# Two groups instead of three in layer 1, and a denser schedule of gathers and last layernorms

## The chip, the cores and the metric

One core of a Trainium2 chip runs the whole program. Its engines have queues of their own and run beside each other: TensorE (PE; its weight loads are PEld), VectorE (DVE), ScalarE (ACT), GpSimd (POOL) and SyncE (SP), which only starts transfers. Plain DMAs are started from SP and ACT, indirect ones (scatter and gather of rows by an index tensor) from POOL. Each engine takes its instructions in the program's order and waits at the head of its queue. The metric is the device time of one execution in microseconds (us).

## What is computed

Two transformer layers over 16 batches of 512 tokens with 128 channels, all in float32. Each layer is a retention attention and a mixture of eight experts, two of them for every token; after each half a layernorm of the sum with its input:

```python
x = _layernorm(x + _L0_attn_ref(x, ...))
x = _layernorm(x + _L0_ffn_ref(x, ...))   # 8 experts, inner width 256, top 2 per token
x = _layernorm(x + _L1_attn_ref(x, ...))
x = _layernorm(x + _L1_ffn_ref(x, ...))   # 8 experts, inner width 512, top 2 per token
```

The expert half of layer 1, the one that the change touches most, computes for every token only its two experts in the kernel:

```python
top_v, top_i = jax.lax.top_k(xf @ Wg, 2)
top_w = softmax(top_v)
y = einsum('enf,efd->end', silu(xf @ W1) * (xf @ W3), W2)
out = sum(take_along_axis(y, top_i) * top_w)
```

## The kernel before

**Groups, parts, blocks.** The batches of a layer are cut into groups (`PARTS`, line 29: layer 0 has two groups of 8, layer 1 three groups of 6, 8 and 2 batches), and a group into parts of 2 or 3 batches. When the attention of a batch is done, its tokens are routed: eight indirect DMAs (`put` in `route`, line 465) scatter its rows into the group's `rows` in DRAM, where every expert has a region of its own. When a part's batches have been routed, `sort` makes a table of blocks of 128 rows on VectorE, each of one expert, and `experts` runs over them. `_blocks` says how many: a part may leave rows of an expert that do not fill a block to the next part; the last part of a group takes all that are left, and so each group has E - 1 = 7 blocks more than its rows would fill. In layer 1 the groups have 9 + 16 + 30, 17 + 24 + 30 and 23 blocks.

**A block** in `experts` takes three loads on SP's queue (the rows `xb` 64 KB, and in layer 1 the weights `w` 512 KB and `wd` 256 KB), a transpose on TensorE (`turn`, line 1007) with its copy on ScalarE (line 1009), in layer 1 eight matmuls up (line 1024), a silu on ScalarE (1032), a product on VectorE (1033), four matmuls down (1043), a copy on ScalarE (1047) and a store into `results` from ScalarE's queue. Blocks go in pairs, with loads two pairs ahead. In float32 each of the matmuls up and down is two records in the profile.

**Gather and layernorm.** A group's results can be used only when its last part is done: then the places of its rows are known (`places`, VectorE work that is spread over the steps of the last part) and the group is `ready`. For a batch, `gather` asks for eight indirect DMAs into a buffer `yg` (three buffers, `YG`) and loads the kept input `xk` on SP's queue (four buffers). `combined` multiplies by the weights on VectorE (line 1101), adds (1106, 1107) and runs the `layernorm`: statistics, `inv_std` and `nb` on VectorE, four activations on ScalarE (line 340). In layer 0 the result is the input of layer 1's attention; in layer 1 `final` stores it to the output from ScalarE's queue.

**The order of work** is made by the loop at the end of `two_layers`. Three slots hold attentions of batches as generators; `order` fixes which comes next. A round goes once over the slots; for each it takes one step of the attention, one indirect DMA off the queue `moves` (`move`, which makes the DMA wait for the last marked instruction, a copy or silu of ScalarE or a product of VectorE, so that it is paced by these), and steps of `queue[0]`, the experts, as `pace` says. After the slots, `fetch` asks for the next batch's gathers if its group is ready and fewer than 2 (layer 0) or, without attention, 3 (layer 1) batches are held, and one step of the first of `finals` is taken. Where no attention is left (`moved` is false), a round is two steps of the experts, each followed by two indirect DMAs:

```python
        if not moved:
            for _ in range(2):
                step()
                move(now=True)
                move(now=True)
        fetch()
        if finals and next(finals[0], finals) is finals:
            finals.pop(0)
```

A scheduler in the framework then places the instructions on each engine's queue, so that the order on an engine isn't exactly that of the calls.

**`r`** (lines 812 and 947) is the sum that goes into the layernorm behind the attention, with eight columns for the router: `[P, C, DE]`, in the pool `ap` with two buffers. It is written from PSUM (by ScalarE in layer 0, line 819, by VectorE in layer 1, lines 953 and 954) and read until the four activations of line 340.

Of the kernel before, what the change touches and what calls it, by code (L numbers as in the profile page):

```python
# [10 lines left out]
F32 = mybir.dt.float32  # L11
# [7 lines left out]
P = 128  # L19
# [6 lines left out]
OVER = 20  # L26


PARTS = ((2, 2, 2, 2), (2, 2, 2, 2)), ((2, 2, 2), (3, 3, 2), (2,))
WAITS = "for indirect DMAs"  # L30
BK = 128
H0, DK0, DV0 = 4, 32, 64
# [6 lines left out]
def _region(B, T):  # L39

    return BK + max(sum(parts) for layer in PARTS for parts in layer) * T

# [91 lines left out]
def two_layers(  # L134
# [22 lines left out]
    C = T // P  # L157
# [3 lines left out]
    RS = _region(B, T)  # L161
    assert all(sum(sum(parts) for parts in layer) == B for layer in PARTS)

# [3 lines left out]
    ap = ctx.enter_context(tc.tile_pool(name="ap", bufs=2))  # L167
# [29 lines left out]
    DE = D + E  # L197
# [34 lines left out]
    def depends(later, earlier, reason):  # L232
        tc.add_manual_dep(
            later.ins,
            earlier.ins.name,
            mybir.DependencyInfo(mybir.DependencyClass.Sync, mybir.DependencyReason.DATA),
            reason=reason,
        )
# [4 lines left out]
    def move(now=False):  # L243

        some = moves[0] or moves[1]
        if not some or not (marks or now):
            return
        begun = some.popleft()()
        if marks:
            last[:] = marks[-1:]  # L250
            marks.clear()
        if last:
            depends(begun, last[0], "paced by the other engines")
# [39 lines left out]
    def two_banks(name):  # L293

        banks = [psum_a(f"{name}_{k}")[:, : 2 * DE].rearrange("p (c d) -> p c d", d=DE) for k in range(2)]
        return banks, [banks[c // 2][:, c % 2] for c in range(C)]
# [48 lines left out]
    class Group:  # L345


        def __init__(self, l, g, begin):
            self.layer, self.name = l, f"{l}_{g}"
            self.parts = PARTS[l][g]  # L350
            self.begin = begin
# [341 lines left out]
    def attention0(b, xT, group):  # L693
        n = f"a0_{b}"
# [114 lines left out]
        if not sums_of:  # L809
            prepare(0)  # L810
        banks, py = two_banks(f"py_{n}")
        r = ap.tile([P, C, DE], F32, tag="r", name=f"r_{n}")
        for c in range(C):
            at = bass.ts(c, P)
            nc.tensor.matmul(py[c], xT[:, at], same0, start=True, stop=False)
# [13 lines left out]
    def attention1(b, xt, group):  # L829


        n = f"a1_{b}"
# [111 lines left out]
        give("v")  # L944
        yield
        banks, py = two_banks(f"py_{n}")
        r = ap.tile([P, C, DE], F32, tag="r", name=f"r_{n}")
        for c in range(C):
            nc.tensor.matmul(py[c], oT[:, bass.ts(c, P)], w2_sb, start=True, stop=True)
            if c % 2:  # L950
# [117 lines left out]
    def gather(l, b):  # L1068

        group = groups[l, b]  # L1070
        k = b - group.begin
        place = group.place[:, k].rearrange("p k c -> p (k c)")
        y = ap.tile([P, 2, C, D], F32, bufs=YG, tag="yg", name=f"yg_{l}_{b}")
        rows = y.rearrange("p k c d -> p (k c) d")
        here = [0]

        def get(n):
            here[0] += 1
            return nc.gpsimd.indirect_dma_start(  # L1079
                out=rows[:, n],  # L1080
                out_offset=None,
                in_=group.results,
                in_offset=bass.IndirectOffsetOnAxis(ap=place[:, n : n + 1], axis=0),
            )

        moves[1].extend(partial(get, n) for n in range(2 * C))
        xt = xp.tile([P, C, D], F32, bufs=YG + 1, tag="xk", name=f"xk_{l}_{b}")
        nc.sync.dma_start(out=xt.rearrange("p c d -> p (c d)"), in_=kept[l, b])
        return y, xt, here
# [24 lines left out]
    for l in range(2):  # L1114
        b = 0
        for g, parts in enumerate(PARTS[l]):
            begin = b
# [7 lines left out]
    def fetch():  # L1125

        for l, most in ((0, 2), (1, 1 if jobs else YG)):
            b = fetched[l]
            held = sum(1 for k, _ in gathered if k == l)
            if b < B and groups.get((l, b)) in ready and held < most:  # L1130
                gathered[l, b] = gather(l, b)
                fetched[l] += 1

    def attention(l, b):
        group = groups[l, b]
        if l == 0:
            yield from attention0(b, xTs.pop(b), group)
        else:
            while (0, b) not in gathered:
                yield WAITS  # L1140
            x2 = yield from combined(0, b, "x2")
            yield
            yield from attention1(b, x2, group)
# [10 lines left out]

    order = [(0, b) for b in range(sum(PARTS[0][0]) + W)]
    later = [(0, b) for b in range(len(order), B)], [(1, b) for b in range(B)]
# [8 lines left out]
    queue, finals = [], []  # L1165
# [3 lines left out]
    def work(group, part, table, blocks, need):  # L1169
        while len(group.puts) < need:  # L1170
            yield WAITS
        last = part == len(group.parts) - 1
        others = places(group) if last else iter(())
        for _ in experts(group, part, table, blocks, group.puts[:need]):
            next(others, None)
            yield
        for _ in others:
            pass
        if last:
            ready.add(group)  # L1180
            if group.layer == 1:
                finals.append(final(group))
# [8 lines left out]
    def pace():  # L1191


        most, so_far = 0.0, 0
        for l, _, some, group in queue:
            so_far += some
            if l == 0 and len(group.runs) == len(group.parts):
                before = until((1, group.begin), 0) - (W * 2 - 1) * STEPS[0] // 2 - OVER // 2
                most = max(most, so_far / max(before, 1))
        ends = {part_of[n][0]: n for n in order}  # L1200
        coming = [until(n, STEPS[0]) for part, n in ends.items() if left[part]]
        if coming:
            most = max(most, so_far / (min(coming) + OVER))
        return most

    def step():

        if queue:
            got = next(queue[0][1], queue)
            if got is queue:  # L1210
                queue.pop(0)
            elif got is not WAITS:
                queue[0][2] -= 1
# [4 lines left out]
    while jobs or any(slots) or queue or finals:  # L1218
        moved = held = False
        for k in range(W):  # L1220
            if slots[k] is None and jobs and steps >= k * STEPS[0] / W:
                l, b = jobs[0]
                if l == 0 or groups[0, b] in ready:
                    jobs.pop(0)
                    if (l, b) not in groups:
                        (_, g, _), begin = part_of[l, b]
                        group = Group(l, g, begin)
                        for i in range(begin, begin + group.size):
                            groups[l, i] = group
                    slots[k] = ((l, b), attention(l, b))  # L1230
                else:
                    held = True
            if slots[k] is None:
                continue
            moved = True
            steps += 1
            move()
            (l, b), gen = slots[k]
            got = next(gen, slots)
            todo[l, b] = max(todo[l, b] - 1, 1)  # L1240
            if got is WAITS or len(moves[0]) + len(moves[1]) > 2 * C:
                move(now=True)
            if got is slots:
                slots[k] = None
                todo[l, b] = 0
                part, _ = part_of[l, b]
                left[part] -= 1
                if not left[part]:
                    group = groups[l, b]
                    i, table, blocks, need = sort(group)  # L1250
                    at = 1
                    while at < len(queue) and queue[at][0] <= l:
                        at += 1
                    some = (blocks + 1) // 2 + (blocks if l else (blocks + 1) // 2)
                    queue.insert(at, [l, work(group, i, table, blocks, need), some, group])
            owed += pace()
            while queue and owed >= 1.0:
                owed -= 1.0
                step()
            if not queue:  # L1260
                owed = 0.0
        if held:
            step()
        if not moved:
            for _ in range(2):
                step()
                move(now=True)
                move(now=True)
        fetch()
        if finals and next(finals[0], finals) is finals:  # L1270
            finals.pop(0)


_OUT = "out_dram"
# [69 lines left out]
```

## Time and profile before

| what | value |
|---|---|
| median of 13 executions | 1500.35 us (1492.54 to 1514.79) |
| the profiled execution | 1502.49 us |
| its span in the profile | 1500.4 us, 34347 instructions |
| TensorE busy | 1286.5 us (86%) |
| weight loads busy | 1120.0 us (75%) |
| VectorE busy | 966.5 us (64%) |
| ScalarE busy | 546.6 us (36%) |
| GpSimd busy | 507.0 us (34%) |
| DMA | 277.36 MB, mean 185 GB/s |
| indirect scatters (line 465) | 256, 999 ns each |
| indirect gathers (line 1079) | 256, 977 ns each |

The profile is one execution. Its busy times are means over stages that differ, so it is read by stages: the part with 40 slices shows which engine is busy when, the stretches in microseconds show it finer, the timeline of one engine gives each instruction with the idle time before it and what ended this, and the groups by line give the mean time of an instruction. A wait for several things is put down to the one that came last. Names in the views have their numbers left out, so `yg` stands for the buffers of all batches; `rout` is `results`, `rin` is `rows`.

### The profile page before, as it was taken

Reading aid. Unit: us, or ns where it says so; the run is one execution under the profiler, and the core shown is the slowest. Engines: PE = TensorE matmul, PEld = TensorE weight load, DVE = VectorE, ACT = ScalarE, POOL = GpSimd, SP = SyncE. Lnnn points to the kernel's source line nnn. Section 1 sums busy time; section 2 is a strip of 40 time slices with the busy share of each in tenths; the row PEclk is TensorE's granted clock in tenths of the full one; section 3 lists DMA queues with packets and bytes.
Section 4 is the critical chain, followed back from the end, with each engine's and each line's share of the span. In section 5 each row is a group of like instructions: output and inputs, shape, how many; then the busy total and the mean of one; then the engine's idle time right before and its main releaser. Section 6 shows DMA issues by size and latency. Waiting matters only on the chain.

```text
span 1500.4 us, 34347 instructions
## 1 busy us (share of the span) xinstructions
PE 1286.5 (86%) x11230; PEld 1120.0 (75%) x11230; DVE 966.5 (64%) x4134; ACT 546.6 (36%) x1344; POOL 507.0 (34%) x519
## 2 busy tenths in 40 slices
PE   6878799999879989879999889999999988887850
PEld 4757678788756868767788779888888987776740
DVE  4685778846665868786658755675877881112465
ACT  3333344434333434514434342452444332222231
POOL 0041320420264341632434523352565340005564
PEclk9889899999989999989999999999999999998985
DMA  5024255566553443627676765775787797788862
GB/s 167 8 85 125 72 159 158 167 194 192 168 164 104 130 123 113 197 69 209 190 254 215 229 206 182 245 238 176 237 266 231 246 304 263 258 254 265 261 200 70
DMA packets 208914, 277.36 MB, mean 185 GB/s; under 512 B 26976, under 2 KB 133728, under 8 KB 208608
## 3 DMA queue, kind: packets, MB, share of 16 engines
q1 hardware_dynamic: 134336, 205.59, 43.9%
q10 hardware_dynamic: 58016, 36.00, 7.7%
q0 software_dynamic: 16384, 33.59, 6.9%
q8 instruction: 89, 1.46, 0.4%
q14 instruction: 89, 0.73, 0.2%
HBM read 224.02 MB, written 51.05 MB: 183 GB/s over the span
## 4 chain that ended last, share of the span: by engine, by line
PE 59%; DVE 15%; DMA 10%; issue 6%; POOL 4%; ACT 3%; SPq 2%; ACTq 0%; POOLq 0%; DVEq 0%
PE pgu L1024 19%; PE py L1043 10%; DMA xb<-rin 5%; POOL yg L1079 4%; PE po_a L778 4%; PE pb_a L707 3%; PE psc_a L656 3%; PE po_a L911 2%; PE pt L1007 2%; DMA yg<-rout,place 2%; PE pa_a L705 2%; DVE sc_a L660 2%; PE py_a L817 2%; PE po_a L770 2%; PE pa_a L847 1%
## 5 line engine op out<-in xcount | busy, mean ns | idle before, releaser
L1024 PE MATMUL pgu<-xbT,w 128*128 128x128 f32 x3520 | 465.2, 285 | 33.4 <-ACT xbT L1009 31.7
L1024 PEld LDWEIGHTS pgu<-xbT,w 128*128 128x128 f32 x3520 | 439.3, 200 | 49.9 <-ACT xbT L1009 39.3
L465 POOL DMA_INDIRECT rin<-x,at_f x256 | 255.8, 999 | 590.1 <-ACT yb L1047 98.5
L1079 POOL DMA_INDIRECT yg<-rout,place x256 | 250.2, 977 | 389.5 <-DMA xb<-rin 136.9
L1033 DVE TENSOR_TENSOR h<-sg,pgu 128x512 f32<-128x512 f32 (+1 forms) x221 | 150.8, 682 | 279.6 <-PE pgu L1024 265.9
L1043 PE MATMUL py<-wd,h 128*128 128x128 f32 x1760 | 242.9, 284 | 18.0 <-ACT xbT L1009 8.0
L1043 PEld LDWEIGHTS py<-wd,h 128*128 128x128 f32 x1760 | 217.1, 194 | 40.2 <-ACT xbT L1009 13.6
L1032 ACT ACTIVATE sg<-pgu 128x512 f32<-128x512 f32 (+1 forms) x221 | 131.3, 594 | 200.9 <-PE pgu L1024 191.4
L660 DVE TENSOR_TENSOR sc_a<-psc_a,cs 128x512 f32<-128x512 f32 x192 | 119.6, 682 | 29.1 <-PE psc_a L656 28.8
L1047 ACT COPY yb<-py 128x256 f32<-128x256 f32 (+1 forms) x148 | 54.4, 368 | 210.7 <-PE py L1043 206.4
L1007 PE MATMUL pt<-cs,xb 128*128 128x128 f32 x291 | 82.3, 297 | 39.2 <-DMA xb<-rin 34.8
L1009 ACT COPY xbT<-pt 128x256 f32<-128x256 f32 (+1 forms) x148 | 54.5, 368 | 124.4 <-PE pt L1007 112.3
L1007 PEld LDWEIGHTS pt<-cs,xb 128*128 128x128 f32 x291 | 41.4, 147 | 59.3 <-DMA xb<-rin 42.3
L778 PEld LDWEIGHTS po_a<-v_a,sc_a 128*128 128x128 f32 x512 | 71.8, 203 | 10.8 <-DVE sc_a L660 5.9
L340 ACT ACTIVATE y_c<-yg,nb_y_c,rs_y_c 128x128 f32<-128x128 f32 x128 | 54.3, 484 | 58.1 <-DVE nb_y_c L334 57.9
L778 PE MATMUL po_a<-v_a,sc_a 128*128 128x64 f32 x512 | 70.8, 279 | 4.4 <-DVE sc_a L660 4.4
L707 PE MATMUL pb_a<-w_in_sb,xT 128*128 128x512 f32 x128 | 70.5, 634 | 0.0
L340 ACT ACTIVATE x<-r_a,nb_x,rs_x 128x128 f32<-128x128 f32 x128 | 54.0, 485 | 20.4 <-DVE nb_x L334 10.3
L786 DVE TENSOR_TENSOR og_a<-po_a,sg_a 128x256 f32<-128x256 f32 x64 | 27.0, 422 | 47.8 <-ACT sq_a L785 47.2
L1101 DVE TENSOR_TENSOR yg<-yg,gw 128x1024 f32<-128x1024 f32 x32 | 39.2, 1226 | 26.2 <-DMA yg<-rout,place 24.8
L656 PE MATMUL psc_a<-qkT_a,kk_a 32*128 32x128 f32 x1024 | 52.9, 290 | 3.0 <-DVE sc_a L660 1.2
L705 PE MATMUL pa_a<-w_in_sb,xT 128*128 128x256 f32 x128 | 42.7, 417 | 13.2 <-DMA w_in_sb<-in_w_in_dram 10.8
(198 smaller groups left out, 1942.6 us busy)
## 6 DMA issues: line engine op xcount, KB each, us to landing
w<-in_ex_dram SPq DMA_DIRECT2D x149, 512.0 KB
wd<-in_ex_dram SPq DMA_DIRECT2D x149, 256.0 KB
w<-in_ex_dram SPq DMA_DIRECT2D x142, 256.0 KB
xb<-rin SPq DMA_DIRECT2D x291, 64.0 KB
rout<-yb ACTq DMA_DIRECT2D x143, 128.0 KB
wd<-in_ex_dram SPq DMA_DIRECT2D x142, 128.0 KB
kept<-x ACTq DMA_DIRECT2D x32, 256.0 KB
xk<-kept SPq DMA_DIRECT2D x32, 256.0 KB
```

Of the source, the lines that this page charges most:

```text
L340: nc.scalar.activation(y[:, c, :], r[:, c, :D], AF.Identity, bias=nb[:, c : c + 1], scale=rs[:, c : c + 1])
L465: moved = nc.gpsimd.indirect_dma_start(out=group.rows, out_offset=bass.IndirectOffsetOnAxis(ap=at[:, n : n + 1], axis=0), in_=xt[:, n % C, :],
L656: nc.tensor.matmul(banks[r][i], kT(r, i), qT(r, i), start=True, stop=True)
L660: return nc.vector.tensor_tensor(sc[:, r], bank.rearrange("p (c t) -> p c t", t=P), causal[:, None, :].to_broadcast([P, C, P]), ALU.mult,)
L707: nc.tensor.matmul(pb, lhsT, w_in0_sb[:, 2 * P :], start=True, stop=True)
L778: nc.tensor.matmul(po[:, h * DV0 : (h + 1) * DV0], sc[:, h, c], v[:, c, h * DV0 : (h + 1) * DV0], start=c == 0, stop=c == 0 or h == H0 - 1,)
L1007: nc.tensor.transpose(pt[:, k], loaded_[i][0], ident)
L1024: nc.tensor.matmul(bank[:, m * nf + f], loaded_[i][1][:, k * F + f * P : k * F + (f + 1) * P], turned[i], start=True, stop=True,)
L1032: mark(nc.scalar.activation(sg, banks[0], AF.Silu))
L1033: nc.vector.tensor_tensor(h, sg, banks[1], ALU.mult)
L1043: nc.tensor.matmul(py[:, m], h[:, f], wd[:, f * P : (f + 1) * P], start=f == 0, stop=f == nf - 1)
L1079: return nc.gpsimd.indirect_dma_start(out=rows[:, n], out_offset=None, in_=group.results, in_offset=bass.IndirectOffsetOnAxis(ap=place[:, ...
```

## The change

Layer 1 has one group of 14 batches, with the parts 2, 2, 2, 3, 3, 2, and one of 2 batches. Its blocks are 9 + 16 + 16 + 24 + 24 + 30 and 23. The region of an expert in `rows` grows with the largest group (`_region`), for both layers. `r` has one buffer. Where no attention is left, each of a round's two expert steps is followed by three indirect DMAs and a `fetch`, and a round takes three steps of the last layernorms instead of one.

```diff
-PARTS = ((2, 2, 2, 2), (2, 2, 2, 2)), ((2, 2, 2), (3, 3, 2), (2,))
+PARTS = ((2, 2, 2, 2), (2, 2, 2, 2)), ((2, 2, 2, 3, 3, 2), (2,))
...
-        r = ap.tile([P, C, DE], F32, tag="r", name=f"r_{n}")
+        r = ap.tile([P, C, DE], F32, bufs=1, tag="r", name=f"r_{n}")
...
-        r = ap.tile([P, C, DE], F32, tag="r", name=f"r_{n}")
+        r = ap.tile([P, C, DE], F32, bufs=1, tag="r", name=f"r_{n}")
...
         if not moved:
             for _ in range(2):
                 step()
-                move(now=True)
-                move(now=True)
+                for _ in range(3):
+                    move(now=True)
+                fetch()
         fetch()
-        if finals and next(finals[0], finals) is finals:
-            finals.pop(0)
+        for _ in range(1 if moved else 3):
+            if finals and next(finals[0], finals) is finals:
+                finals.pop(0)
```

## The prediction

> **What bounds the kernel now.** First the page's second part, the span in 40 slices, to see where the engines change places:
>
> ```profile
> PE   6878799999879989879999889999999988887850
> ...
> POOL 0041320420264341632434523352565340005564
> ```
>
> TensorE is at 90% or more through most of the span. GpSimd is at a third, has nothing at all in slices 34 to 36, and works on at the end, where TensorE has run dry. So the last stages were cut out with the busy times by stretch (columns: stretch, its length, then PE, PEld, DVE, ACT, POOL busy with counts, TensorE's clock, DMA share, GB/s):
>
> ```profile
> 1075.00:1125.00 50.00, 46.24 (x455) 41.08 (x455) 40.24 (x155) 19.62 (x46) 31.74 (x33) 1.00 0.77 251
> 1125.00:1175.00 50.00, 49.64 (x563) 43.31 (x562) 39.16 (x149) 20.23 (x52) 26.66 (x28) 1.00 0.72 230
> 1175.00:1235.00 60.00, 54.12 (x464) 51.95 (x463) 51.10 (x258) 24.01 (x56) 25.20 (x26) 1.00 0.90 288
> 1235.00:1355.00 120.00, 101.05 (x838) 94.80 (x837) 22.70 (x33) 32.71 (x68) 0.00 (x0) 1.00 0.80 258
> 1355.00:1449.00 94.00, 72.11 (x545) 66.74 (x542) 38.66 (x116) 26.80 (x61) 51.77 (x52) 0.93 0.80 260
> 1449.00:1500.40 51.40, 0.00 (x0) 0.00 (x0) 32.93 (x137) 9.97 (x25) 28.92 (x29) 0.51 0.26 79
> ```
>
> Three stages: until 1235 attention, experts and the final layernorms of group 1_0's six batches lie together, TensorE 150.0 of 160 us busy. From 1235 to 1355 the last 30 blocks of group 1_1 run alone. From 1355 the gathers of 1_1 and 1_2 run, at first beside the 23 blocks of 1_2, from 1449 with TensorE idle. GpSimd's timeline of that end (start, duration, what, idle before and its releaser):
>
> ```profile
> 1355.41 0.97 POOL L1079 DMA_INDIRECT yg<-rout,place  x1 [122.62 <-DMA xb<-rin]
> 1356.69 0.96 POOL L1079 DMA_INDIRECT yg<-rout,place  x1 [0.30 <-issue]
> ...
> 1379.19 0.94 POOL L1079 DMA_INDIRECT yg<-rout,place  x1 [5.38 <-ACT yb L1047]
> ...
> 1426.80 0.94 POOL L1079 DMA_INDIRECT yg<-rout,place  x1 [7.16 <-ACT y_c L340]
> ...
> 1444.01 0.94 POOL L1079 DMA_INDIRECT yg<-rout,place  x1 [6.63 <-ACT xbT L1009]
> ...
> 1486.14 0.95 POOL L1079 DMA_INDIRECT yg<-rout,place  x1 [0.30 <-issue]
> ```
>
> A gather takes 0.94 us and the next starts 0.30 later. 80 gathers stand between 1355.41 and 1486.14, the start of the last. In the undisturbed end, from 1455.65 to 1486.14, 23 pitches take 30.49 us: 1.326 each (some gathers stretch to 1.1 to 1.8 us). 79 such pitches would be 104.7; the stretch has 130.7, so 26 us are stalls, all before 1454. From the last gather's start to the span's end are 14.3 us: 3.0 to land, 6.2 of VectorE, 1.65 of ScalarE, the store. The end is bound by GpSimd's chain of gathers, everything before by TensorE.
>
> **The change, part by part.** *Blocks.* Every last part of a group has 7 blocks of padding more (`_blocks`): layer 1 falls from 55 + 71 + 23 = 149 to 119 + 23 = 142. A block's price, from the page's fifth part:
>
> ```profile
> L1024 PE MATMUL pgu<-xbT,w 128*128 128x128 f32 x3520 | 465.2, 285 | 33.4 <-ACT xbT L1009 31.7
> ...
> L1043 PE MATMUL py<-wd,h 128*128 128x128 f32 x1760 | 242.9, 284 | 18.0 <-ACT xbT L1009 8.0
> ...
> L1007 PE MATMUL pt<-cs,xb 128*128 128x128 f32 x291 | 82.3, 297 | 39.2 <-DMA xb<-rin 34.8
> ```
>
> Layer 1's block has 16, 8 and 1 of them: 16 x 0.132 + 8 x 0.138 + 0.28 = 3.5 us busy. In the clean stretch two blocks come every 7.23 us (starts 1250.33 and 1257.56), 3.6 each. Seven blocks: 25 us, at least 21 (32 matmuls in 3.84 us, so 0.12 each). In the changed program's order they are gone from before the last attention: TensorE's queue reaches that point 91 matmuls earlier (13 a block), the 30 and 23 blocks behind it stay.
>
> *Final layernorms out of the middle.* Six batches leave the stretch that ends at 1235: 48 gathers (60 us of GpSimd), 6 x 6.2 = 37 us of VectorE (first multiply 1489.15 to `nb` 1495.3), 6 x 1.65 = 10 of ScalarE. TensorE is idle for only 3.8 + 0.4 + 5.9 = 10 us of that stretch, and its own work stays, so this gives back 0 to 10: I take 4, since the idle time stands mostly before blocks whose rows or weights are late (DMA 0.90 in the last 60 us), which lighter VectorE does not load. The scatters behind those gathers on GpSimd come earlier; that helps only the same 10 us. The larger `sort` and `places` (27 more instructions of three kinds, 0.29 to 0.35 each, some 9 us, where the order puts them between the `h` of the previous part) lie on VectorE where two final layernorms (12 us) are gone; without that cover they'd cost up to the 5.9.
>
> *One buffer for `r`.* From its first write (L819, L953) to its last read (L340) `r` lives 6.5 to 13.6 us in the trace; put in the order of the batches, seven pairs overlap, by 3.8, 6.5, 3.3, 3.3, 3.9, 3.1 and 2.7 us, together 27. The second of a pair then waits, and holds its two PSUM banks; other slots and experts fill TensorE. 0 to 27, I take 3: near nothing, since TensorE is 85 to 97% busy there, in stretches of 100 us from 500 to 1100. It can gain nothing.
>
> So the first gather of the end comes 25 + 4 - 3 = 26 us earlier, at 1329.4 (17 to 35).
>
> *The end.* Group 1_0 now has 14 batches, ready only after its last part. Nothing is gathered for layer 1 before: 112 + 16 = 128 gathers stand behind that point instead of 80. 127 pitches of 1.326 are 168.4 us, 48 of them (63.6) new. Three moves a step let GpSimd have 9 gathers a pair of blocks: 11.9 us against 7.23, so GpSimd, not pacing, is the bound, unless it waits.
>
> *Stalls.* Before, 26 us in 57 gathers beside the experts, 0.46 each: there one final step a round put a batch's multiply on VectorE rounds after its gathers, and the fourth batch's gathers waited for that buffer (7.16, 6.63). With three steps it comes at once. What remains is read from the changed order: which gather (numbered from the first of the end) stands behind which batch's ScalarE output. From a batch's eighth gather to the end of its `y` are 3.0 to 5.8 us to land (5.8 beside experts: 1364.54 to the multiply at 1370.32), 6.2 VectorE, 1.65 ScalarE. Mostly 10 to 17 gathers (13 to 22 us) lie between, enough. Short are: gather 57, behind `y` of batch 4, which VectorE finishes only after batch 5's multiply (gather 51): 12.7 to 15.5 needed, 8.0 there, 5 to 7.5 lost; gather 79 behind batch 7, whose `nb` stands behind batch 8's multiply (gather 75): 6.1 to 8.9 against 5.3, 1 to 3.6; gather 105 behind batch 10 and batch 11's multiply (gather 96): 0 to 3. Sum 6 to 14: I take 10; ends 0, and 44 at the old rate over the 97 gathers beside experts. On SP's queue the `xk` loads of batches 4 to 11 now stand before weights of blocks 10 to 22; each waits for the add of the batch four before it, done by then, and behind it would wait weights that are loaded two pairs (14 us) ahead. ScalarE's `y` and stores stand between `xbT`, `silu` and `yb` of the 23 blocks; delays there are the stalls counted.
>
> *Sum.* 1329.4 + 168.4 + 10 + 14.3 = 1522.1, with 2.1 outside the span (1502.49 against 1500.40) 1524.2. That execution lay 2.1 above the median of 13 (1500.35), so 1522.
>
> Two rules of the skill bear on this. The Trainium skill's page "Perfetto Trace Analysis", Optimization Strategy, says that where the most contended engine changes over time, interleaving the regimes can help; the change does the reverse, it takes GpSimd's work from TensorE's stage into its own. By it alone the sum would be the 64 us of new pitches against the 25 of blocks. The page "SBUF — State Buffer", section on the two sides (the "DVE blocks DMA" trap), has descriptor writing on GpSimd locked out while VectorE holds the shared port. The trace shows stretched gathers, 1.79 us at 1460.73 beside a multiply begun at 1460.48, but per final only 30.49 - 23 x 1.25 = 1.7 over three, 0.6 each. Were each multiply and its two adds (1.23 + 0.69 + 0.69) a full lock, 16 finals would cost 42 instead of 10, and the sum would be 1554.
>
> **Rivals.** *The middle is held by the final layernorms, not TensorE* (faster): for it speaks VectorE at 51.1 of 60 us in the last stretch; against it TensorE's 150 of 160. If all 37 us of VectorE came back, the gain would be 25 + 37 - 3 = 59, not 26: 1489. It decides the sign from 26 of the 37 on. *ScalarE, VectorE and SP couple GpSimd to the experts as before*: extra moves wait for marks, stalls stay 0.46 a gather: 44 instead of 10, 1556. For it: 26 us of such waits now, and VectorE takes in finals ahead of the experts' `h`. Against: gathers are early there, buffers free sooner. Where three moves simply do nothing, this is the result too. *The single `r` holds PSUM*: 27 instead of 3, 1546; against it: other slots run.
>
> **How the numbers follow.** Forecast 78%, finals in the middle 8, coupling 10, `r` 4. The range: gain 35 and no stall give 1503; gain 17 and stalls of 29 give 1550. Two executions of this kernel apart by less than 0.3% (4.5 us) can't be told apart. Faster than that: 6 of the first rival's 8. Within: its other 2 and 4 from the forecast's lower edge. Slower: 88%.
>
> **What would show it.** Right: no layer-1 gather before some 1330, the 30-block stretch still at 7.2 us a pair, then 128 gathers at about 1.33 with 5 to 15 us of stalls, TensorE dry for some 45 us at the end, span about 1520. First gather before 1315: the middle was not TensorE's. Stalls over 30 us: coupling. First gather after 1340: `r`. It would be wrong altogether if pitches fell below 1.15, which no row here shows.

## The result, and the profile after

The changed kernel takes 1531.45 us (median of 14 runs, 1528.05 to 1539.29) against 1500.6 of the kernel before beside it: 1.0208 of before, 95% interval 1.0189 to 1.0227. On another occasion it was 1.0197 (1.0164 to 1.0231). The profiled execution took 1530.86 us, its span is 1529.1.

The 40 slices of the changed kernel:

```profile
PE   6869799999879889889898998999999988856540
...
POOL 0041320420362532532434633524201400067575
```

GpSimd's empty stretch is there as before, three slices long, but what follows is five slices at 5 to 7 tenths instead of four at 4 to 6; and TensorE, which held 7 and 8 tenths beside the gathers before, now falls to 4 to 6. GpSimd's timeline (start, duration, what, idle time before and its releaser) has the numbers:

```profile
1341.32 0.97 POOL L1079 DMA_INDIRECT yg<-rout,place  x1 [125.46 <-DMA w<-in_ex_dram]
1342.60 0.96 POOL L1079 DMA_INDIRECT yg<-rout,place  x1 [0.30 <-issue]
...
1420.11 0.94 POOL L1079 DMA_INDIRECT yg<-rout,place  x1 [5.59 <-DVE rs_y_c L322]
...
1451.77 0.94 POOL L1079 DMA_INDIRECT yg<-rout,place  x1 [3.76 <-ACT y_c L340]
...
1514.72 0.94 POOL L1079 DMA_INDIRECT yg<-rout,place  x1 [0.30 <-issue]
```

The end's first gather is 14.1 us earlier than before (1355.41), its last 28.6 later (1486.14): 128 gathers in 173.4 us where 80 took 130.7. Only two waits over 2 us are left; the two lines show 5.59 and 3.76 where 0.30 is the usual idle time, 8.8 us together. The rest is (173.4 - 8.8) / 127 = 1.296 a gather. From the last gather's start to the end are 14.4 us.

The two stages of this end (stretch, its length, PE, PEld, DVE, ACT, POOL busy with counts, TensorE's clock, DMA share, GB/s), from the first gather to the last matmul, and behind it:

```profile
1341.00:1476.00 135.00, 83.15 (x530) 78.06 (x528) 71.33 (x265) 36.33 (x83) 96.37 (x98) 0.78 0.69 221
1476.00:1529.00 53.00, 0.22 (x2) 0.00 (x0) 29.05 (x125) 10.14 (x25) 30.52 (x31) 0.50 0.26 76
```

The last 23 blocks, 530 records here and 545 before, take 135 us instead of 94, and TensorE is busy for 83 of them. That did not set the end: GpSimd's gathers ran on behind them without a pause of more than 2 us. But it is a new stall, and the experiments show what it does where less work covers it.

### The profile page after: what moved, and what is told of

The parts are those of the page before. It is cut to its first block, busy times and chain, and to the rows that moved or that the text cites. A ratio compares the mean times of both kernels' runs of the same rounds, so it can differ in the third digit from the quotient of the medians.

```text
span 1529.1 us, 33854 instructions
## 1 busy us (share of the span) xinstructions
PE 1286.7 (84%) x11055; PEld 1117.2 (73%) x11055; DVE 976.4 (64%) x4160; ACT 541.1 (35%) x1329; POOL 510.2 (33%) x519
## 4 chain that ended last, share of the span: by engine, by line
PE 50%; DVE 14%; DMA 8%; issue 5%; POOL 4%; ACT 3%; SPq 2%; ACTq 0%; POOLq 0%; DVEq 0%
PE pgu L1024 17%; PE py L1043 9%; DMA xb<-rin 4%; POOL yg L1079 4%; PE psc_a L656 2%; PE po_a L911 2%; DMA yg<-rout,place 2%; PE po_a L778 2%; PE pa_a L847 2%; DVE h L1033 2%; PE pt L1007 2%; DVE sc_a L660 2%; PE pb_a L707 2%; PE pr_a L935 1%; PE po_a L770 1%
## 5 line engine op out<-in xcount | busy, mean ns | idle before, releaser
L1024 PE MATMUL pgu<-xbT,w 128*128 128x128 f32 x3408 | 453.5, 286 | 39.7 <-ACT xbT L1009 37.4
L1024 PEld LDWEIGHTS pgu<-xbT,w 128*128 128x128 f32 x3408 | 428.0, 201 | 56.5 <-ACT xbT L1009 45.4
L1033 DVE TENSOR_TENSOR h<-sg,pgu 128x512 f32<-128x512 f32 (+1 forms) x214 | 145.9, 682 | 242.5 <-PE pgu L1024 233.2
L1043 PE MATMUL py<-wd,h 128*128 128x128 f32 x1704 | 243.7, 289 | 42.4 <-DVE h L1033 33.5
L1032 ACT ACTIVATE sg<-pgu 128x512 f32<-128x512 f32 (+1 forms) x214 | 127.3, 595 | 195.9 <-PE pgu L1024 176.0
L1047 ACT COPY yb<-py 128x256 f32<-128x256 f32 x144 | 53.1, 368 | 207.1 <-PE py L1043 204.9
L1007 PE MATMUL pt<-cs,xb 128*128 128x128 f32 x284 | 79.1, 296 | 38.9 <-DMA xb<-rin 35.9
L1009 ACT COPY xbT<-pt 128x256 f32<-128x256 f32 x144 | 53.1, 369 | 131.1 <-PE pt L1007 118.0
L705 PE MATMUL pa_a<-w_in_sb,xT 128*128 128x256 f32 x128 | 43.1, 420 | 13.1 <-DMA w_in_sb<-in_w_in_dram 10.7
```

What stands on the lines that cost most here:

```text
L1007: nc.tensor.transpose(pt[:, k], loaded_[i][0], ident)
L1024: nc.tensor.matmul(bank[:, m * nf + f], loaded_[i][1][:, k * F + f * P : k * F + (f + 1) * P], turned[i], start=True, stop=True,)
L1032: mark(nc.scalar.activation(sg, banks[0], AF.Silu))
L1033: nc.vector.tensor_tensor(h, sg, banks[1], ALU.mult)
L1043: nc.tensor.matmul(py[:, m], h[:, f], wd[:, f * P : (f + 1) * P], start=f == 0, stop=f == nf - 1)
```

## The experiments

The kernels ran in three sets, each on one chip beside the kernel before, and chips differ: the kernel before took 1638.8 us beside the first set, 1499.0 beside the second and 1505.8 beside the third. Why they differ isn't known. So times are read as ratios to the kernel before of the same set.

**First set: the parts of the change alone.** The single `r` in the kernel before (lines 812 and 947), the denser end in the kernel before, the changed kernel with two `r`, and only the larger regions:

```diff
-        r = ap.tile([P, C, DE], F32, tag="r", name=f"r_{n}")
+        r = ap.tile([P, C, DE], F32, bufs=1, tag="r", name=f"r_{n}")
```

> The kernel before with one buffer for r in place of two, and nothing else. Theory (the single r is the mis-sized term: the first gather of the end came at 1341.3 where 1329.4 was forecast, and the changed kernel falls behind by about 10 us between 490 and 690 us, where lifetimes of r of two batches overlap): 8 to 13 us longer than before, 1508 to 1514, and the sorts of layer 1's first parts 7 to 13 us later. Rival 1 (the larger regions of rows, or the order of the scatters that follows from the new parts, cost these 10 us): 1499 to 1502. Rival 2 (the 27 us of overlap all come out as time): 1524 to 1530.

> The kernel before with only the denser end (three indirect DMAs a step and a fetch, three steps of the last layernorms a round); three groups and two buffers for r as before. By the forecast's account of the end, GpSimd's chain bounds it: first gather at 1355, 79 pitches of 1.30 to 1.33 = 103 to 105, stalls 5 to 10 in place of 26, 14.4 behind: 1478 to 1484. Rival 1 (the stalls come from the coupling of ScalarE and VectorE to the experts, and more moves a step only wait more often): 1497 to 1503. Rival 2 (last layernorms ahead of the experts' products make TensorE's 23 blocks end later than before and these bind): over 1503.

```diff
-        gt = sp.tile(some, F32, bufs=1, tag="pos", name=f"gtn_{n}")
+        gt = sp.tile(some, mybir.dt.bfloat16, bufs=1, tag="pos", name=f"gtn_{n}")
...
-        r = ap.tile([P, C, DE], F32, bufs=1, tag="r", name=f"r_{n}")
+        r = ap.tile([P, C, DE], F32, tag="r", name=f"r_{n}")
```

> The changed kernel with two buffers for r again. To make room, the comparison in sort that counts blocks (0 or 1 a value) is kept in bf16, 0.9 KB less in a partition; the result is the same and its price is a few tenths of a us at most. Theory (the single r costs 8 to 13 us): 1518 to 1524, first gather of the end at 1328 to 1333. Rival (larger regions, or the order that follows from the parts): 1530 to 1533, first gather at 1341.

```diff
-    return BK + max(sum(parts) for layer in PARTS for parts in layer) * T
+    return BK + 14 * T
```

> The kernel before with regions of rows for 14 batches in place of 8 (7296 rows an expert in place of 4224), as the changed kernel has them; no other edit. Theory (the single r costs the 10 us): 1499 to 1502. Rival (rows further apart make scatters or loads of rows slower): 1508 to 1514, with scatters on GpSimd over 1.01 us or the loads of rows later.

Measured, as ratios to before: single `r` 1.0043 (1.0009 to 1.0077), denser end alone 1.0105 (1.0060 to 1.0151), changed kernel with two `r` 1.0134 (1.0084 to 1.0184), regions alone 1.0041 (1.0014 to 1.0069). The absolute forecasts miss, since all of them were made for a chip like that of the result. Of the ratios, the single `r` and the regions cost the same 7 us here, so this set does not tell the theory from its rival (the comparison of the changed kernel with one and with two `r` follows in the second set). What is clear is the denser end: it made the kernel before slower, where the forecast's account had it 16 to 22 us faster.

**Second set: the changed kernel, with two `r`, and with the old end; and another end for the kernel before.** The second kernel is the third of the first set.

> The changed kernel itself, as the measure for the three that run beside it (on the chip of the first four experiments the kernel before took 1639 us and not 1500, so only ratios to the kernel before on the same chip, and differences between kernels of one call, are read). On a chip like the first: 1.019 to 1.023 of before. On the slower one: 1.015 to 1.025.

> The changed kernel with two buffers for r (the same kernel as e3_new_two_r). Theory (the single r costs 8 to 13 us of the middle): 0.5% to 0.9% below the changed kernel beside it, its first gather of the end 8 to 13 us earlier. Rival (the order from the new parts, or the regions, cost the 12 us): within 0.2% of the changed kernel. Second rival (r's wait is real, but a chip at a lower clock hides it): below 0.3% on the slow chip only.

```diff
-                for _ in range(3):
-                    move(now=True)
-                fetch()
+                move(now=True)
+                move(now=True)
         fetch()
-        for _ in range(1 if moved else 3):
-            if finals and next(finals[0], finals) is finals:
-                finals.pop(0)
+        if finals and next(finals[0], finals) is finals:
+            finals.pop(0)
```

> The changed kernel with the old end: two indirect DMAs a step, no fetch between, one step of the last layernorms a round. By the prediction's account (stalls at the old 0.46 us a gather without the denser end, 10 us with it): 30 to 40 us longer than the changed kernel, 1.04 to 1.05 of before. Rival, from the experiment with the denser end alone (1.0105 of before; VectorE's queue held the experts' products behind multiplies that waited for gathers, 31 us of TensorE's waits for h): the denser end only moves the stall from GpSimd to TensorE. With 128 gathers TensorE has time to spare, so that it still pays, but less: 10 to 25 us. If it does nothing: within 0.3% of the changed kernel.

```diff
         for b in range(group.begin, group.begin + group.size):
             while (1, b) not in gathered:
                 yield
+            while queue and b + 1 < group.begin + group.size:
+                if (1, b + 1) in gathered and gathered[1, b + 1][2][0] >= LAG:
+                    break
+                yield
             y = yield from combined(1, b, "x2")
...
                 move(now=True)
                 move(now=True)
+                fetch()
         fetch()
-        if finals and next(finals[0], finals) is finals:
-            finals.pop(0)
+        for _ in range(1 if moved else 3):
+            if finals and next(finals[0], finals) is finals:
+                finals.pop(0)
```

The last kernel (against the kernel before, `LAG` is 5) also lets `fetch` hold five batches once no attention is left, two of each five in buffers of the attention's tags `v` and `g`.

> The kernel before (three groups, two buffers for r, two indirect DMAs a step) with an end in which the multiply of a batch is put on VectorE only after five gathers of the next batch have been issued, three steps of the last layernorms a round and a fetch each step; two further buffers for gathered rows and kept inputs are the attention's v and g, which are free by then. Theory (TensorE's wait for h in the denser end comes from multiplies that hold VectorE's queue while their gathers are under way; GpSimd's stalls in the kernel before come from too few free buffers): waits of TensorE for h under 10 us and stalls of GpSimd under 10 us at once, and a time of 0.985 to 0.993 of before. Rival (the 23 blocks of the last part bind the end whatever the order): 0.997 to 1.003.

Measured: 1526.92 (1.0197; 1.0164 to 1.0231), 1514.45 (1.0102; 1.0074 to 1.0130), 1546.55 (1.0324; 1.0291 to 1.0357) and 1477.79 us (0.9860; 0.9819 to 0.9901).

*Two `r`.* The first and the last gather of the changed kernel in this set, and then of the kernel with two buffers:

```profile
1341.45 0.97 POOL L1079 DMA_INDIRECT yg<-rout,place  x1 [123.33 <-DMA w<-in_ex_dram]
...
1511.62 0.94 POOL L1079 DMA_INDIRECT yg<-rout,place  x1 [0.30 <-issue]
```

```profile
1329.31 0.97 POOL L1079 DMA_INDIRECT yg<-rout,place  x1 [123.41 <-DMA w<-in_ex_dram]
...
1501.31 0.94 POOL L1079 DMA_INDIRECT yg<-rout,place  x1 [0.30 <-issue]
```

The stage before the gathers is 12.1 us shorter with two buffers, the time 12.5. Both kernels have the larger regions and the new parts, so the rival, which put the 12 us on these, falls. (The edit also keeps a comparison in bf16, to make room; the third set has the single `r` without that.) On this chip the regions cost little in any case: up to the eleventh sort, near 820 us, the sorts of the kernel with two buffers start within some 4 us of those of the kernel before. On the chip of the first set they cost 0.4%; why isn't known. The busy times of one stretch of the middle, of the changed kernel and then with two buffers, show the changed kernel falling behind:

```profile
500.00:1000.00 500.00, 457.94 (x4219) 391.39 (x4218) 361.25 (x1636) 199.26 (x498) 207.44 (x208) 0.97 0.59 183
```

```profile
500.00:1000.00 500.00, 462.07 (x4354) 397.66 (x4356) 360.32 (x1637) 200.13 (x500) 208.12 (x209) 0.97 0.59 187
```

In the same 500 us, at the same clock, TensorE does 135 records less with one `r` (the changed kernel's first profile has 4175 here, so some 40 of them are scatter between executions), but it is idle for only 4 us more. The whole stretch up to the first gather, in which both programs have the same matmuls, shows where the rest is:

```profile
0.00:1341.40 1341.40, 1205.81 (x10521) 1040.59 (x10522) 875.16 (x3771) 494.18 (x1221) 383.45 (x391) 0.95 0.56 176
```

```profile
0.00:1329.30 1329.30, 1194.05 (x10520) 1035.04 (x10521) 867.43 (x3771) 493.59 (x1221) 383.63 (x391) 0.96 0.57 178
```

With one `r` the matmuls take 11.8 us longer, and idle time grows by 0.3 us only (135.6 against 135.3). So in this pair the loss is not waiting but longer matmuls. No write of `r` (lines 819, 953, 954) has an idle time before it that the last reader of the older `r` (line 340) ends: the profile shows no stall in front of that one buffer. The scheduler gave the two programs different orders on TensorE, from 170 us on. The granted clock, 0.95 against 0.96, has the right sign, but these means are too coarse to say how much of the 11.8 us it explains. How the 12 us follow from one buffer stays open.

*The old end.* Its gathers that waited longest, and its last, in the changed kernel with two indirect DMAs a step:

```profile
1406.93 0.94 POOL L1079 DMA_INDIRECT yg<-rout,place  x1 [7.16 <-ACT y_c L340]
...
1424.14 0.94 POOL L1079 DMA_INDIRECT yg<-rout,place  x1 [6.64 <-ACT xbT L1009]
...
1530.20 0.94 POOL L1079 DMA_INDIRECT yg<-rout,place  x1 [0.30 <-issue]
```

From its first gather at 1339.39 to 1530.20 are 190.8 us; 127 x 1.296 = 164.6 leaves 26.2 of stalls, about as many as in the kernel before (28.3 with the same pitch), with the same longest ones (7.16 and 6.64 here, 7.16 and 6.63 there). So the denser end is worth 19.6 us in the changed kernel (1546.55 - 1526.92), which is the rival's 10 to 25 and not 30 to 40.

*The lagged end.* Waits on VectorE and of TensorE for `h` (engine, line, waited for: us in all, times, longest) beside the last 23 blocks, in the changed kernel of the first profile and then in the kernel with the lag:

```profile
DVE yg L1101 <- DMA yg<-rout,place: 41.7, 7, 12.4
...
PE py L1043 <- DVE h L1033: 33.5, 7, 12.2
...
DVE h L1033 <- PE pgu L1024: 17.4, 8, 5.5
```

```profile
DVE h L1034 <- PE pgu L1025: 27.9, 14, 4.9
...
PE py L1044 <- DVE h L1034: 2.5, 4, 1.0
...
DVE yg L1111 <- DMA yg<-rout,place: 0.7, 1, 0.7
```

In the changed kernel VectorE stands for 41.7 us at the head of its queue with a multiply whose gathers are still under way, and the products `h` of the experts stand behind it; TensorE waits 33.5 us for these. In the kernel before the two waits are 6.8 and 7.6 us, so the denser end brought them in. With the multiply put five gathers later they are 0.7 and 2.5 us. (Lines are one more for `h` and ten more for the multiply, since the kernel has new lines.) Its 23 blocks, and its first and last gather:

```profile
1357.00:1444.00 87.00, 68.98 (x531) 63.70 (x531) 51.26 (x170) 29.67 (x67) 65.02 (x64) 0.96 0.90 296
```

```profile
1357.07 0.97 POOL L1086 DMA_INDIRECT yg<-rout,place  x1 [122.95 <-DMA w<-in_ex_dram]
...
1447.20 1.02 POOL L1086 DMA_INDIRECT yg<-rout,place  x1 [4.08 <-DVE rs_y_c L316]
...
1466.26 0.94 POOL L1086 DMA_INDIRECT yg<-rout,place  x1 [0.30 <-issue]
```

64 gathers and 23 blocks pass in the same 87 us; then only the last part's 16 gathers remain. From the first to the last gather are 109.2 us, against 130.7 in the kernel before. This version beats both kernels: 0.986 of before. What the lag, the two further buffers and the denser schedule each have of that was not tried apart.

**Third set: what was open.** One `r` for each layer (tags `r0` and `r`, one buffer each, in the kernel with two); the first set's single `r` and denser end again; and the changed kernel with half of the gathers.

> The changed kernel with one buffer for r for each layer in place of one for both (the comparison in sort in bf16, as in f2_after_two_r, so that it fits). Where the single r's 12 us come from: if from the pairs in which one batch is in layer 0 and the other in layer 1 (overlaps of 3.8 and 6.5 us before), the time is that with two buffers, 1.008 to 1.012 of before; if from pairs within layer 1 (five overlaps of 2.7 to 3.9 us), it is the changed kernel's, 1.018 to 1.022; if from both, between, 1.013 to 1.017.

> The same kernel as e1_single_r (the kernel before with one buffer for r), which gave 1.0043 of before on the slower chip. Theory (the single r costs the same in the kernel before as in the changed one, 12 us): 1.006 to 1.010 on a chip like that of the second call. Rival (it costs only in the new order of parts, where the group's end no longer gives the time back): 0.998 to 1.003.

> The same kernel as e2_tail_only (the kernel before with only the denser end), which gave 1.0105 of before on the slower chip. Theory (the denser end takes GpSimd's 26 us of stalls away, but puts multiplies that wait for their gathers ahead of the experts' products on VectorE; with 80 gathers the last 23 blocks then bind, and the last 16 gathers wait for them): 1.000 to 1.012, with an idle time of over 15 us on GpSimd before the last 16 gathers. Rival (that was the slower chip's doing; the stalls saved come out as time): 0.984 to 0.990.

```diff
-        moves[1].extend(partial(get, n) for n in range(2 * C))
+        moves[1].extend(partial(get, n) for n in range(C if l else 2 * C))
...
+        K = 1 if l else 2
...
-        nc.vector.tensor_tensor(r, r, y[:, 1], ALU.add)
+        if K == 2:
+            nc.vector.tensor_tensor(r, r, y[:, 1], ALU.add)
```

> The changed kernel with half of layer 1's gathers: each last layernorm gathers, weighs and adds the rows of a token's first expert only; the second expert's share of the output is left out. 64 gathers stand at the end in place of 128. Theory (GpSimd's chain of gathers at 1.3 us each bounds the end): the end shrinks until the 23 blocks and the eight gathers behind them bind: first gather at 1341, blocks done some 95 us later, 8 x 1.3 = 10, 14 to the end, 1462 to 1475 us (0.975 to 0.984 of before). Rival (the end is bound by VectorE and ScalarE, with gathers only beside it; VectorE loses 5.2 us a batch less 3.3 here): 1500 to 1515. Second rival (TensorE's blocks bind already): 1520 to 1530.

Measured: 1.0160 (1.0119 to 1.0201), 1.0071 (1.0041 to 1.0101), 1.0112 (1.0076 to 1.0149) and 0.9761 (0.9704 to 0.9817).

*One `r` a layer* lies between the two, where both kinds of pairs were to have a share; but its interval reaches into those of the kernels on either side, so that the shares are not settled.

*The single `r`* in the kernel before costs 10.7 us of 1505.84 (6 to 15), much as in the changed kernel: it does not take the new order of parts, and the rival, 0.998 to 1.003, is out. Its first gather:

```profile
1373.97 0.97 POOL L1079 DMA_INDIRECT yg<-rout,place  x1 [123.28 <-DMA xb<-rin]
```

That is 12.2 us behind the first gather of the kernel with the denser end alone (1361.82, below), which has two `r` and is otherwise the kernel before until no attention is left. Up to there TensorE has 10693 and 10695 records, with 1228.0 us busy against 1218.7: here 9.3 us are longer matmuls and 2.9 idle time.

*The denser end alone* is slower on this chip too. Waits of TensorE for `h` from 1340 on, and GpSimd's first gather of the end, the first of the last 16, and the last:

```profile
PE py L1043 <- DVE h L1033: 28.4, 6, 10.0
```

```profile
1361.82 0.98 POOL L1079 DMA_INDIRECT yg<-rout,place  x1 [123.05 <-DMA xb<-rin]
...
1486.18 0.94 POOL L1079 DMA_INDIRECT yg<-rout,place  x1 [34.16 <-issue]
...
1505.13 0.94 POOL L1079 DMA_INDIRECT yg<-rout,place  x1 [0.30 <-issue]
```

The stalls of GpSimd have become one, 34 us, before the last part's gathers: they wait until its blocks are done, and those end late because TensorE waits 28 us for products that VectorE holds back. "issue" as the releaser says only that the profile shows nothing that was waited for; the last matmul of the 23 blocks ends at 1483.3.

*Half of the gathers.* First and last gather of 64:

```profile
1341.56 0.97 POOL L1079 DMA_INDIRECT yg<-rout,place  x1 [123.31 <-DMA xb<-rin]
...
1451.34 1.02 POOL L1079 DMA_INDIRECT yg<-rout,place  x1 [0.30 <-issue]
```

With the start of the end where it was (1341.56 against 1341.32 and 1341.45), the time is 1468.69 us, inside the first theory's 1462 to 1475 and far from both rivals. GpSimd's chain of gathers sets the changed kernel's end.

## Why the prediction was right, and where not

The forecast was 1522 us in a range of 1503 to 1550, slower; it came to 1531.45. By its steps:

- **Blocks and final layernorms out of the middle (25 + 4 of 26).** With two `r` the first gather comes 1355.4 - 1329.3 = 26.1 us earlier than in the kernel before; 29 were forecast for the two together. They were not tried apart. The 30-block stretch stayed at 7.23 us a pair, as said.
- **The single `r` (3 taken, 0 to 27).** This step failed in its size: 12.1 us at the first gather, 12.5 in the time, 10.7 in the kernel before. The reason given was that other slots and experts fill a TensorE that is 85 to 97% busy. Idle time did grow little, by 0.3 and 2.9 us in the two pairs; but the same matmuls took 11.8 and 9.3 us longer, which the sum had no term for, and why they did stays open. The sign named for it, a first gather after 1340, came true. In the span, the first gather came 12 us later than forecast (9 by `r`, 3 by the step above), and the chain gave 5 back (next step): 7 us in all, 1529.1 against 1522.1. So the total is nearer than its terms, by luck: misses of both signs partly cancel.
- **The chain (168.4) and its stalls (10).** 164.6 and 8.8. The pitch of 1.326 was taken from the last 23 pitches of the kernel before; in the changed kernel the last 23 are 1.310, and the whole chain without its two long waits has 1.296. Of the three short gathers the first two waited 5.6 and 3.8 (5 to 7.5 and 1 to 3.6 forecast), the third did not (0 to 3). That GpSimd's chain bounds the end is shown by the half gathers.
- **The rival that the denser end does nothing, 44 us of stalls.** With the old end the stalls are 26.2. They do not grow by 0.46 for each further gather beside the experts, as the prediction had it: the long waits stand before the same gathers as in the kernel before (the 15th, 17th, 41st and 49th).
- **The cost that the prediction didn't see.** It looked for what gathers wait for, and not for what waits behind the multiplies. Its line on VectorE's "finals ahead of the experts' `h`" stood with the coupling rival at 10%; the wait is real (TensorE waited 33.5 us for `h`), but in this kernel it lies under 128 gathers. With 80 the denser end as a whole costs 17 us, although it was to take stalls off GpSimd.
- **Rivals of the middle.** Had final layernorms held it, the first gather would have come before 1315, with one `r` or with two. It didn't.

The Trainium skill's page "Perfetto Trace Analysis", Optimization Strategies, holds that TensorE should be kept as busy as can be and that what blocks it is to be mended; the runs agree. The change took 7 blocks off TensorE and lost; the lagged end left all blocks, shortened GpSimd's chain, for which TensorE stands idle at the end (from 51.6 us in the kernel before to 35.9), and gained 1.4%. The prediction weighed, and did not take, 42 us for a lock of GpSimd by the multiplies and adds of 16 last layernorms. The page that it named, "SBUF — State Buffer", has that lock for VectorE's two-port modes and says that a `tensor_tensor`, which the multiply and the adds are, has no such mode and, with both inputs in SBUF, contends with GpSimd's reads alone. Starts of undisturbed gathers are 1.25 apart, and (1.296 - 1.25) x 127 = 5.8 us is all that the chain has above that beside its two long waits, so no full lock is seen.

## What to carry to other kernels

Where work is moved behind a point, price it by the engine that bounds the stage where it arrives: 48 gathers at 1.3 us in GpSimd's own stage weigh more than seven blocks saved on TensorE. An instruction that waits at the head of an in-order queue delays all that stands behind it (here VectorE's 41.7 us of waits for gathers went with 33.5 us of TensorE's), so try issuing the consumer of a transfer some steps after the transfer, with a buffer more, and not as soon as the program allows. A buffer taken away from a stage that is bound can cost time even where no wait on that buffer is seen, as 12 us here.

## What was not expected of the hardware

TensorE's granted clock fell with its waits. Beside the same 23 blocks it was 0.93 before, 0.78 in the changed kernel and 0.96 with the lagged end, and a record of a matmul took 72.11 / 545 = 132 ns, 83.15 / 530 = 157 and 68.98 / 531 = 130. So a wait seems to cost twice, once as idle time and once in the matmuls around it; no run here changes the clock alone. With TensorE idle the mean is 0.50. (The Trainium skill's page "TensorE: Matmul & The Clock Gate", Part 1, has a gate with a half and a full rate that follows the activity of the last microseconds; the means here agree with that.)

And chips differ by 9% on the same kernel: the kernel before with a single `r` had a span of 1645.5 us at a mean clock of 0.911 on one chip and 1515.5 at 0.935 on another, with gathers of 977 ns on the one and 981 ns on the other. Why the first is slower isn't known.
